# Residual through the w transforms of a spectral block, run as four 64x64 tiles, in an attention and FFT kernel

## The chip, the cores and the metric

The kernel runs on one core of one Trainium2 chip. The metric is device microseconds, the median over runs of one launch. Before the change it is 3665.09 us over 3 runs (3663.27 to 3667.23).

## The reference, cut to what matters

`x` is [2, 48, 48, 768] float32: two images of 48 x 48 pixels (2304 tokens) and 768 channels. Two layers follow each other, each a residual around a group norm (32 groups) and a body:

```python
x = x + attention(_gn(x))      # 12 heads of 64, relative positions in h and w, then @ proj_w + proj_b
x = x + spectral(_gn(x))

def spectral(x):               # B, H, W, C = 2, 48, 48, 768; nb, bs = 8, 96
    xf = rfft2(x, axes=(1, 2), norm='ortho')              # [2, 48, 25, 768], complex
    xr, xi = (p.reshape(B, Hf, Wf, nb, bs) for p in (xf.real, xf.imag))
    o1r = gelu(einsum(xr, w1[0]) - einsum(xi, w1[1]) + b1[0])
    o1i = gelu(einsum(xi, w1[0]) + einsum(xr, w1[1]) + b1[1])
    o2r = softshrink(einsum(o1r, w2[0]) - einsum(o1i, w2[1]) + b2[0], 0.01)
    o2i = softshrink(einsum(o1i, w2[0]) + einsum(o1r, w2[1]) + b2[1], 0.01)
    return irfft2(o2r + 1j * o2i, s=(48, 48), norm='ortho')
```

Each einsum multiplies the 96 channels of one of 8 blocks by a 96x96 matrix. A two-dimensional transform is done as two one-dimensional ones, over w (48 points to 25 complex values) and over h.

## The kernel before

**Order of the work.** Attention for both images comes first (24 pairs of heads, 18 units each). Then, image by image, the output projection with the residual (`project_out`) and the spectral layer (`Spectral`). Nearly all matmuls are float32, which the trace shows as two records per matmul. Instructions are issued to each engine in program order where an `InOrder` wrapper is used (`pr.sync`, `pr.pool`, `self.sync`); the others may be put in another order by a scheduler that works with estimated costs.

**`project_out`, one image.** 18 tiles of 128 tokens, in 6 groups of three. For each group `tokens` loads the attention output `oT` (128 channels on the partitions) and the inverse softmax sums `inv` by SP's queue, and GpSimd multiplies them. For each tile and each half of 384 output channels, `product` accumulates six matmuls in a PSUM bank `acc`. The residual rows of `x` lie in six tiles `x2[i]` of [96, 4, 768]: two image rows of 48 pixels on 96 partitions, four such pairs along the free dimension. `rows(i)` loads one, and GpSimd adds the projection bias `pb`. VectorE adds `acc` into `x2` (L941); since 128 tokens and 96 pixels do not match, `shifts(t)` cuts each `acc` into three pieces (108 adds per image). As soon as two pairs of rows are complete, `over_w` transforms them over w: four matmuls per call with the constant `fw` (96 x 112, block diagonal for the two image rows) on 192 channels of two row pairs, so 384 columns (`ps_y`, L920). ScalarE copies the result to `y1`, and SP stores it to DRAM as `y_d` (L929). For the last tile the two channel halves are transformed and stored one after the other.

**Where things lie.** `x2` stays in SBUF to the end of the image: it also collects the output. For the first image the projection's weights `w`, bias `pb` and two of the three token buffers lie in the large buffer `span`, the first tokens in buffers left from attention; for the second image everything but two token buffers lies in a region `po_r` ("room") which is loaded while the first image's spectral layer ends.

**`Spectral`, one image.** The channels are worked in 8 blocks of 96, `n = 0..7`, two blocks to a slice `s` of 192 channels. `load` brings five pieces `y2` of a slice from `y_d`, which puts h on the partitions. Per block: `over_h` (25 matmuls into `ps_z`, squares for the group norm on ScalarE), `mean` and `norm` (small VectorE operations, among them L1071 and L1073, then the sums `both` on GpSimd), `first` (the block's `w1` in a three-multiplication complex product, Gelu), `second` (`w2`, bias, soft shrink: VectorE makes a clipped value, GpSimd subtracts it, L1177). In the second block of each slice `back_h` follows two pieces behind: the transform back over h (`ps_u`), and a store to `u_d` (L1199). Block n's `over_h(n+1)` runs before `second(n-1)` and `first(n)`.

`back_w(s)` is the transform back over w: for each of six `u2` tiles of [100, 4, 192] it runs two matmuls with `iw` (100 x 96, `ps_x`, L1213), VectorE adds the result into `x2` (L1221), and SP stores those rows of that slice to `out`. It also loads the `u2` tiles of the next slice. It is called at the end of the turns n = 2 (which only loads the tiles of s = 0), 4, 6 and 8 (s = 0, 1, 2), and for s = 3 at the end.

**`prepare`.** `prepare(False)`, at n = 7, opens the second image's projection: first tokens and weights are loaded by SP. `prepare(True)`, before the last `back_w`, runs what is left of its steps.

## Time and profile before

| | |
|---|---|
| median of 3 runs | 3665.09 us (3663.27 to 3667.23) |
| the profiled execution | 3660.19 us, of which its span is 3658.4 |
| mean granted TensorE clock in the span | 0.987 |
| busy: TensorE, VectorE, ScalarE, GpSimd | 97%, 79%, 70%, 56% |
| DMA | 607.61 MB, 166 GB/s over the span |
| attention of both images | 0 to about 2838 us |
| projection of image 0, last `acc` | 2838.0 to 2984.2 |
| first `first` of image 0 | 3010.3 |
| last `ps_x` of image 0 | 3236.5 |
| projection of image 1, last `acc` | 3236.5 to 3405.4 |
| first `first` of image 1 | 3430.0 |
| last store of `u_d`; end of the span | 3634.37; 3658.4 |

How to read the views: PE is TensorE's matmuls, PEld its weight loads (beside the matmuls), DVE VectorE, ACT ScalarE, POOL GpSimd, SP the engine that issues most DMAs. A group's line names the source line, engine, operation, the tiles written and read, the tile shape that TensorE uses (rows*columns), the operand shapes and the count; then the busy time, the mean of one in ns, and the idle time of the engine just before, with what ended it. A row of the chain of waits has its start and duration in us and the engine or DMA that the end of the span waited for. A row of the stretches has its limits and length, the busy time of PE, PEld, DVE, ACT and POOL with instructions in brackets, the granted clock (1 is full speed), the busy share of the 16 DMA engines, and GB/s. Matmul records in a stream overlap, so the mean of one is longer than what one adds to the stream.

### The profile page before, as it was taken

To read this page: it belongs to the slowest core of one execution; us is meant where nothing else is said; L and a number is where in the kernel's file an instruction comes from. 1 tells how busy PE (TensorE), PEld (TensorE's weight loads), DVE (VectorE), ACT (ScalarE), POOL (GpSimd) and SP (SyncE) were. 2 spreads that over 40 slices of the span, in tenths; PEclk is the share of its full clock that TensorE was granted. 3 is DMA by queue.
4 is the path that set the end of the run, shared out by engine and by line. 5 is a ranking of instruction groups with operands and counts; after the bars stand their busy time and mean duration, and the time that the engine had idled before them with its cause. 6 is when DMAs were issued, how large, how long until landed. Compare 5 with 4: busy or idle time off the path is not lost.

```text
span 3658.4 us, 92606 instructions
## 1 busy us (share of the span) xinstructions
PE 3548.6 (97%) x36032; PEld 2477.2 (68%) x36032; DVE 2902.1 (79%) x6771; ACT 2557.2 (70%) x3769; POOL 2047.2 (56%) x662
## 2 busy tenths in 40 slices
PE   7999999999999999999999999999988999999898
PEld 5677676767767666677676767767666557655675
DVE  4798989989989996799898989899996437743576
ACT  3788888888888888688888888888885124301342
POOL 2567666757575763567666666666673524343232
PEclk9999999999999999999999999999999989999999
DMA  3687778777777885677777777777888743585434
GB/s 105 142 181 171 180 171 179 172 179 171 181 169 175 214 200 122 140 178 174 176 176 171 177 173 175 176 176 172 188 190 190 200 127 85 169 213 147 109 110 140
DMA packets 496484, 607.61 MB, mean 166 GB/s; under 512 B 179117, under 2 KB 311597, under 8 KB 496046
## 3 DMA queue, kind: packets, MB, share of 16 engines
q1 hardware_dynamic: 496046, 601.68, 69.3%
q8 instruction: 286, 4.69, 0.6%
q14 instruction: 152, 1.25, 0.1%
HBM read 131.60 MB, written 87.67 MB: 60 GB/s over the span
## 4 chain that ended last, share of the span: by engine, by line
PE 84%; DVE 5%; ACT 3%; DMA 3%; issue 2%; POOL 1%; SPq 1%; POOLq 0%; DVEq 0%; ACTq 0%
PE ps_o L68 22%; PE ps_s L68 21%; PE ps_proj L68 15%; PE ps_v L68 8%; PE acc L68 7%; DVE s L68 2%; PE ps_u L1195 2%; PE ps L1160 2%; PE ps_y L920 2%; PE ps_r L68 2%; SPq L68 1%; PE ps_x L1213 1%; DMA pT<-s 1%; ACT spectrum L1035 1%; POOL s L68 1%
## 5 line engine op out<-in xcount | busy, mean ns | idle before, releaser
L68 POOL TENSOR_TENSOR s<-rhw 128x2304 f32<-128x2304 f32 x432 | 1740.8, 4062 | 1025.3 <-DMA pT<-s 546.8
L68 DVE CUSTOM_DVE_ANT_0 s<-ps_s,s 128x512 f32<-128x512 f32 (+1 forms) x2160 | 1222.2, 633 | 299.7 <-issue 196.1
L68 ACT ACTIVATE s<-s,nm 128x1152 f32<-128x1152 f32 x864 | 1074.7, 1245 | 335.3 <-DVE nm L68 333.1
L68 DVE STREAM_TRANSPOSE s<-s 128x1152 f32<-128x1152 f32 x864 | 1112.0, 1344 | 6.8 <-ACT s L68 6.8
L68 ACT COPY pT<-s 32x1152 f32<-32x1152 f32 x864 | 993.6, 1150 | 25.9 <-PE ps_o L68 7.5
L68 PE MATMUL ps_o<-pT,v 128*64 128x128 f32 x15552 | 906.5, 276 | 41.7 <-ACT res L68 18.9
L68 PEld LDWEIGHTS ps_o<-pT,v 128*64 128x64 f32 x15552 | 875.4, 139 | 84.0 <-issue 43.6
L68 PE MATMUL ps_s<-kT,qT 64*128 64x512 f32 (+1 forms) x4320 | 899.8, 554 | 4.9 <-DVE mx L68 1.7
L68 PEld LDWEIGHTS ps_s<-kT,qT 64*128 64x128 f32 x4320 | 432.3, 186 | 418.1 <-issue 347.0
L68 PE MATMUL ps_proj<-xnT,w 128*64 128x384 f32 (+1 forms) x4032 | 591.3, 446 | 4.9 <-ACT xnT L68 3.7
L68 PEld LDWEIGHTS ps_proj<-xnT,w 128*64 128x64 f32 x4032 | 281.0, 137 | 278.8 <-issue 212.1
L941 DVE TENSOR_TENSOR x<-acc,x 32x384 f32<-32x384 f32 (+2 forms) x216 | 119.2, 553 | 227.8 <-PE acc L68 163.8
L68 PE MATMUL ps_v<-w,xnT 128*64 128x128 f32 x5184 | 297.3, 274 | 0.0
L68 PEld LDWEIGHTS ps_v<-w,xnT 128*64 128x64 f32 x5184 | 281.7, 137 | 21.2 <-DVE mx L68 21.2
L927 ACT COPY y<-ps_y 112x384 f32<-112x384 f32 x96 | 46.0, 479 | 299.5 <-PE ps_y L920 282.7
L68 DVE DVE_READ_ACCUMULATOR2_ANT mx<- 128x1 f32 x2160 | 179.7, 83 | 0.0
L68 ACT ACTIVATION_READ_ACCUMULATOR s<-s,nm 128x1 f32 x864 | 161.4, 187 | 0.0
L1177 POOL TENSOR_TENSOR spectrum<-spectrum 128x480 f32<-128x480 f32 x80 | 96.3, 1204 | 113.2 <-DVE spectrum L1176 85.0
L1160 PE MATMUL ps<-w,spectrum 96*64 96x96 f32 x3200 | 143.1, 248 | 0.0
L1160 PEld LDWEIGHTS ps<-w,spectrum 96*64 96x64 f32 x3200 | 133.6, 137 | 11.1 <-issue 4.4
L68 PE MATMUL acc<-proj_s 128*128 128x384 f32 x360 | 118.2, 486 | 0.4 <-POOL x L68 0.4
L68 PEld LDWEIGHTS acc<-proj_s 128*128 128x128 f32 x360 | 68.3, 190 | 48.2 <-POOL x L68 0.6
(139 smaller groups left out, 2299.8 us busy)
## 6 DMA issues: line engine op xcount, KB each, us to landing
pT<-s SPq DMA_DIRECT2D x2592, 144.0 KB
t<-rel SPq DMA_DIRECT2D x144, 189.0 KB
rhw<-t SPq DMA_DIRECT2D x144, 144.0 KB
y<-y_d SPq DMA_DIRECT2D x40, 360.0 KB
u_d<-spectrum SPq DMA_DIRECT2D x40, 360.0 KB
u<-u_d SPq DMA_DIRECT2D x48, 300.0 KB
w<-in_qkv_w SPq DMA_DIRECT2D x36, 384.0 KB
oT<-res SPq DMA_DIRECT2D x72, 192.0 KB
```

The source lines that it names most:

```text
L68: return lambda *args, **kw: self.tc.keep_in_program_order(op(*args, **kw))
L920: nc.tensor.matmul(ps[:YP, : 2 * SC], lhsT=k.fw, rhs=part[:, t0 : t0 + 2, ch], start=True, stop=True,)
L927: nc.scalar.copy(y1[:, :, ch], ps[:YP, : 2 * SC].rearrange("p (t c) -> p t c", c=SC))
L941: nc.vector.tensor_tensor(dst, acc[p : p + n, :UQ], dst, ALU.add)
L1035: self.nc.scalar.activation(junk, part, AF.Square, accum_out=total)
L1160: nc.tensor.matmul(ps[64 * r : 64 * r + 64, w * BS : (w + 1) * BS], lhsT=self.o1[:, ri, f0 : f0 + 64], rhs=w2[:, (0, 2, 1, 0)[2 * r + ri], ...
L1177: nc.gpsimd.tensor_tensor(val, val, clip, ALU.subtract)
L1195: nc.tensor.matmul(ps[: 2 * HW, :480], lhsT=k.ih, rhs=d2[:, c0 : c0 + 480], start=True, stop=True)
L1213: nc.tensor.matmul(ps[: 2 * HW, : 2 * SC], lhsT=k.iw, rhs=self.u2[s, i][:, t : t + 2, :], start=True, stop=True,)
```

## The change

The residual is no longer kept in SBUF. The transform over w and the one back over w give the identity together, so the transformed residual `yy`, which is read again from `y_d`, is added to `u2` before the transform back, and its result is the output.

- **Layout.** An image row lies on 64 partitions instead of 48: of each pair of rows, row 0 on partitions 0 to 47, row 1 on 64 to 95 (its first 32 pixels) and 112 to 127 (the others), the last 16 pixels of both rows lie side by side on 32 to 63 and again on 96 to 127, and `fw` is zero for the copy that a row does not use. `rows` loads a group of eight image rows with five DMAs (48, 16, 32, 16, 16 partitions) into a tile [128, 4, 768], three buffers in rotation. In attention the token order within a group is changed to match (`finish`, `send`, the latter with two more DMAs); the last group of the last pair and its inverse sums go by ScalarE's queue. `moves` cuts three to five pieces of an `acc` (156 adds per image).
- **Forward.** `fw` is 64 wide, twice on the partitions. Each `over_w` does, for each half of 384 channels, two by two matmuls on 64x64 tiles: input rows 0 to 63 and 64 to 127, output columns 0 to 63 and 64 to 127 (8 matmuls of 384 columns instead of 4). ScalarE copies and, itself, issues two stores of 50 partitions. For the last group the three tiles' first halves come first, then their second halves, with the `over_w` calls between; only the last call, on half the channels, stands behind the last product.
- **Backward.** `u2` and `yy` are [128, 8, 192] tiles, three each for the whole kernel, image row parity on the upper and lower 64 partitions, each loaded by two DMAs of 50 partitions (`fetch`). For s = 0 to 2 GpSimd adds `yy` to `u2` (`residual`: three adds of 128x1536 at n = 3, 5, 7), one turn after the loads; the transform follows at the next `back_w`, whose results are copied by VectorE and ScalarE in turn to `ot` tiles (three buffers) and stored by two DMAs per tile. For s = 3 the sum is made in PSUM: `yy` and `u2` are both multiplied and accumulated, for two or three pairs of banks with `yy` ahead of `u2` (`early`).
- **Around it.** GpSimd's clips and `both` are issued in program order; `mean(0)` and `norm(0)` come one piece earlier in image 0's and image 1's `over_h(1)`; the constants are loaded once; `y2` has 10 buffers instead of 8; the second image's `w` and `pb` change places in the region; two product halves of the second image run in `prepare(True)`; six GpSimd fills clear the new tiles once.

```diff
 def moves(t):
+    done = 0
+    for p in range(0, P, 32):
+        k, m = divmod(t % 3 * 4 + p // 32, 3)
+        if p >= done:
+            n = min(P, p + 96 - 32 * m) - p if p in (0, 64) and m == 0 else 32
+            yield p, n, k, 32 * m
+            done = p + n
+        if m == 1:
+            yield p, 32, k, 96
...
     def rows(g):
-        part = x2[i]
-        pr.sync.dma_start(out=part, in_=x_v[:, i * XP : (i + 1) * XP, :])
-        for j in range(XP):
-            pr.pool.tensor_tensor(part[:, j, :], part[:, j, :], pr.pb[:R], ALU.add)
+        part = rows_pool.tile([P, 4, C], F32, tag="x1", name="x1")
+        x1[g] = part
+        sync = nc.sync if pr.room is not None and g < 2 else pr.sync
+        for q, i, w0, n in (
+            (0, 0, 0, 48), (48, 1, 32, 16), (64, 1, 0, 32), (96, 0, 32, 16), (112, 1, 32, 16),
+        ):
+            sync.dma_start(out=part[q : q + n], in_=x_v[g, i, w0 : w0 + n])
+        for j in range(4):
+            pr.pool.tensor_tensor(part[:, j, :], part[:, j, :], pr.pb, ALU.add)
...
+    def over_w(n, halves=range(2)):
+        g, k0 = n // 2, 2 * (n % 2)
+        y1 = work.tile([P, 2, C], F32, tag="y1", name="y1")
+        for hf in halves:
+            cols = slice(hf * UQ, (hf + 1) * UQ)
+            both = [bank(f"ps_y{i}") for i in range(2)]
+            for c in range(2):
+                for i in range(2):
+                    r = slice(64 * i, 64 * i + 64)
+                    pr.pe.matmul(
+                        both[i][64 * c : 64 * c + 64, :UQ],
+                        lhsT=k.fw[r, :],
+                        rhs=x1[g][r, k0 + c, cols],
...
+            for i in range(2):
+                nc.scalar.copy(y1[:, i, cols], both[i][:, :UQ])
+        cols = slice(halves[0] * UQ, (halves[-1] + 1) * UQ)
+        for c in range(2):
+            nc.scalar.dma_start(
+                out=y_v[2 * n + c, :, :, cols], in_=y1[64 * c : 64 * c + 2 * KW, :, cols]
             )
-        pr.sync.dma_start(out=y_d[:, 2 * g : 2 * g + 2, ch], in_=y1[:, :, ch])
...
+    for t in range(NT - 3):
...
+        if t % 3 == 2:
+            over_w(2 * g)
+        elif t % 3 == 0 and g:
+            over_w(2 * g - 1)
+    c = HW // 4 - 1
+    for hf in range(2):
+        for t in range(NT - 3, NT):
+            outputs(t, hf)
+            if t == NT - 3:
+                if hf:
+                    over_w(c, (0,))
+                else:
+                    over_w(c - 2)
+        over_w(c - 1, (hf,))
+    over_w(c, (1,))
...
+    def fetch(self, tiles, src, j):
+        for i in range(2):
+            self.sync.dma_start(
+                out=tiles[j][64 * i : 64 * i + 2 * KW], in_=src[i][..., j * XP : (j + 1) * XP, :]
+            )
+
+    def rows_of(self, j, q, both, terms, first=True, last=True):
+        pe, k = InOrder(self.tc, self.nc.tensor), self.k
+        for x, of in enumerate(terms):
+            for m in range(2):
+                for i in range(2):
+                    r = slice(64 * i, 64 * i + 2 * KW)
+                    t = XP // 2 * m + 2 * q
+                    pe.matmul(
+                        both[i][64 * m : 64 * m + 64, : 2 * SC],
+                        lhsT=k.iw[r, :],
+                        rhs=of[j][r, t : t + 2, :],
+                        start=first and x == 0,
+                        stop=last and x == len(terms) - 1,
...
     def back_w(self, s, more, early=0):
+        last = s == NBK // NB - 1
...
+        if more:
+            ch = slice((s + 1) * SC, (s + 2) * SC)
+            u_v = self.u_d.rearrange("w (i r t) c -> i w r t c", i=2, r=2)
+            for j in parts:
+                self.fetch(self.yy, self.y_d.rearrange("(q i) t c -> i q t c", i=2)[..., ch], j)
+        for j in parts if s < 0 else ():
+            self.fetch(self.u2, u_v, j)
+        for turn in turns[:early]:
+            ahead[turn] = banks()
+            self.rows_of(*turn, ahead[turn], [self.yy], last=False)
+        for j, q in turns:
...
+                self.rows_of(j, q, both, [self.yy, self.u2] if last else [self.u2])
...
+            for i in range(2):
+                self.copy(
+                    ots[j][:, 2 * q : 2 * q + 2, i, :],
+                    both[i][:, : 2 * SC].rearrange("p (t c) -> p t c", c=SC),
                 )
...
+                if more:
+                    self.fetch(self.u2, u_v, j)
+                for m in range(2):
+                    self.sync.dma_start(
+                        out=self.out_v[j, m, :, :, s * SC : (s + 1) * SC],
+                        in_=ots[j][64 * m : 64 * m + HW].rearrange("p t i c -> p (t i) c"),
+                    )
+    def residual(self):
+        for u2, yy in zip(self.u2, self.yy):
+            self.pool.tensor_tensor(u2, u2, yy, ALU.add)
...
             elif i == 0:
                 self.back_w(s - 2, True)
-        self.prepare(True)
-        self.back_w(s - 1, False)
+            elif s:
+                self.residual()
+        held = self.prepare(True)
+        self.back_w(s - 1, False, early=2 if held else 3)
```

## The prediction

> **What bounds the kernel now.** I read the page first (which engine carries the chain), then stretches of the span, the groups by form, the chain of waits in time order, and single lines and DMA answers for prices.
>
> ```profile
> span 3658.4 us, 92606 instructions
> ...
> PE 3548.6 (97%) x36032; PEld 2477.2 (68%) x36032; DVE 2902.1 (79%) x6771; ACT 2557.2 (70%) x3769; POOL 2047.2 (56%) x662
> ...
> PE ps_o L68 22%; PE ps_s L68 21%; PE ps_proj L68 15%; PE ps_v L68 8%; PE acc L68 7%; DVE s L68 2%; PE ps_u L1195 2%; PE ps L1160 2%; PE ps_y L920 2%; PE ps_r L68 2%; SPq L68 1%; PE ps_x L1213 1%; DMA pT<-s 1%; ACT spectrum L1035 1%; POOL s L68 1%
> ```
>
> TensorE is the chain, and attention (up to about 2838 us) is most of it. The change works in the last 820 us, where its targets `ps_y` and `ps_x` stand on the chain. The stretches of the two output projections, the first entry into the spectral stage, and the tail:
>
> ```profile
> 2838.00:2984.20 146.20, 144.91 (x449) 83.99 (x450) 53.00 (x96) 21.08 (x45) 59.16 (x33) 1.00 0.65 167
> 3236.30:3405.40 169.10, 167.95 (x521) 97.47 (x520) 58.08 (x106) 21.09 (x44) 67.76 (x29) 1.00 0.69 166
> ```
> ```profile
> 2975.00:3000.00 25.00, 19.59 (x98) 13.79 (x97) 6.54 (x12) 8.64 (x21) 2.18 (x3) 0.89 0.73 187
> 3000.00:3025.00 25.00, 21.43 (x153) 16.66 (x152) 13.43 (x42) 14.69 (x37) 5.10 (x5) 0.70 0.30 75
> ...
> 3625.00:3658.40 33.40, 24.86 (x104) 11.15 (x102) 17.64 (x32) 2.22 (x4) 2.41 (x2) 0.98 0.68 212
> ```
>
> Columns are PE, PEld, DVE, ACT, POOL busy, clock, DMA share, GB/s. The projections are TensorE-bound at full clock with DMA at 0.65 to 0.69; the entry loses both busy time and clock (0.70); the tail is moved by DMA at 212 GB/s.
>
> ```profile
> L920 PE MATMUL ps_y<-x,fw 96*112 96x384 f32 x192 | 66.8, 487 | 4.6 <-DVE x L941 4.6
> L1213 PE MATMUL ps_x<-u,iw 100*96 100x384 f32 x192 | 66.7, 499 | 7.9 <-DMA u<-u_d 6.6 <-DVE x L1221 1.3
> ```
> ```profile
> 2989.11 5.27 DMA y<-y_d
> 2994.52 6.56 PE ps_z L1100 x40
> 3019.03 4.33 PE ps_z L1100 x50
> ```
> ```profile
> 3103.19 1.78 PE ps_u L1195 x4
> 3117.91 7.74 PE ps_x L1213 x24
> ```
>
> From the chain: a 384-column record takes 7.74/24 = 0.3225 us in a stream, and a matmul is two records, 0.645 us. `ps_z` at the entry costs 0.164 us a record against 0.087 later: the low clock.
>
> **1. Forward w transforms.** Before, an image has 48 matmuls (96 records): 31.0 us on TensorE. After, 96 matmuls on 64x64 tiles, 192 records. How many run side by side is not in this trace for four tiles; for two it is:
>
> ```profile
> 1001.59 2.42 PE L68 MATMUL ps_s<-kT,qT 64*128 64x512 f32 x10
> ```
>
> Ten 512-column records alone would need 10 x 0.430 = 4.3 us; two row halves together took 2.4. With four at once 192 x 0.3225/4 = 15.5 us; with two, 31.0 again. I take four, since row halves (`ps_s`) and column halves (`ps_proj`, 4032 records in 591 us, 0.147 each) both overlap fully. A switch of shape costs: four `ps_u` records of 480 columns should take 1.61 us and took 1.78 between `ps` column halves, so (1.78 - 1.61)/2 = 0.085 per switch; 28 switches per image at just under 0.1 are 2.7 us. [...] Gain: 2 x (31.0 - 15.5 - 2.7) = **-25.6** (bounds -26 and +5).
>
> Beside it, hidden: DVE adds rise from 108 to 156 per image at 0.553 us (L941), 86 us in 133; with no such room the extra 27 us would count. ScalarE issues 28 stores at SP's 0.3 to 0.4 us, 10 us beside 21 busy. Six zero fills on GpSimd lie between 0.1 us (the 96x32 fill) and 48 times that each, at most 35 us beside 59 of 146. In attention two more small DMAs per `send`, 24 times, are 38 us of SP's queue over 2800 us (three took 2.40), and nobody waits for `inv_d` soon. Constants of the second image are no longer loaded, which was off the chain.
>
> **DMA cover.** The new transfers touch 48, 50, 32 or 16 partitions instead of 96 to 128. In one group's 17 us (rates in 40 slices):
>
> ```profile
> GB/s 220 394 398 231 29 148 311 329 361 351 249 192 184 202 184 184 239 253 206 220 192 221 184 217 206 224 231 239 267 224 210 224 224 239 275 405 412 419 328 275
> ```
>
> The `oT` tokens on 128 partitions run at 310 to 400, the `inv` broadcast on 64 at 184 to 250, `x` on 96 at 206 to 267, the 112-partition `y_d` store at 400. [...] Rows alone: 32-partition `pT` copies ran at 222 GB/s, so 16 partitions lie between 222 and half that. Of `x` (1.57 MB per group) the 48- and 32-partition pieces, 0.98 MB, take 4.4 us, the three of 16, 0.59 MB, 2.7 to 5.3: 7.1 to 9.7 against 5.2 (1.18 MB at 227). The `y_d` stores (1.23 MB) take 3.4 to 5.6 (360 to 220 GB/s) against 3.4. Six groups add 11 to 40: DMA time per image goes from 0.65 x 146 = 95 us and 0.69 x 169 = 117 to 106..135 and 128..157, against TensorE's 133 and 156. **+6** (0 to +14).
>
> **2. Backward w transforms.** `back_w` for s=0 and 1 stands on the chain at 7.74 us (24 records); after, 48 records at a quarter: 3.9 plus two switches, -3.7. Four times: **-14.8** (+1 if only two tiles overlap). DVE's 12 adds of 0.553 become 12 copies split with ScalarE, less than before. For s=2 and 3 DMA decides, see 5 and 6.
>
> **3. Entry.** Now the last `acc` ends at 2984.2 and 3405.4, `first(0)` starts at 3010.3 and 3430.0. SP holds the loads behind the `y_d` store of the other half (2989.11). After, the store is ScalarE's, and half 0 is finished 9 us of TensorE work earlier: `over_h(0)` and (1), 4.3 us each, and `norm(0)`, 6 us, put `first(0)` 16 us after `acc`: -10. In image 1 four of five pieces share memory with the projection weights and wait for the last product: -5. `mean` and `norm` one piece earlier are in this. **-15** (-8 to -20).
>
> **4. GpSimd adds.** 128x480 takes 1.204 us and 128x2304 5.05, so 128x1536 takes 3.4, three 10.3 us, at n=3, 5, 7. GpSimd is otherwise idle 11 us or more before the next clip at n=3 and 5. But:
>
> ```profile
> L1071 DVE TENSOR_TENSOR nm_rstd<-nm_rstd,nm_fit x48: 145/155/1203, 3007.5 to 3584.1; 96x1 f32<-96x1 f32 x48
> L1073 DVE TENSOR_SCALAR w<-w,nm_rstd x16: 412/416/944, 3009.7 to 3584.8; 96x288 f32<-96x288 f32 x16
> ```
>
> These DVE lines stretch to a GpSimd add's whole length (1203 ns). At n=3 the norm's last L1071 and L1073 (3087.2, 3087.4) follow the last clip (3084.7 to 3085.9), where the adds now start: up to 5.5 us during which `first`'s evictions queue behind them on DVE; seven banks soak up part. I take 2.5 each, four times: **+10** (0 to +20). At n=7 GpSimd is idle 6.75 us before the clip of 3619.18, so it comes 3.5 late, and `back_h` waits: **+3.5** for image 1 (0 to 5); image 0's is in 5.
>
> **5. Handover to image 1.** Now `ps_x` ends at 3236.5, six product halves (3.87 each) carry TensorE to 3259.7. After: two halves run earlier, `ps_x` is shorter, 6 us of TensorE idle can go. Against that DMA carries 3.7 MB of `yy` more (18 us at 200 GB/s), halves of `u` and `out` at two thirds of the speed, and `x` rows: `u` lands 9 to 18 us later than 3235, then four halves: 3261 to 3270, and up to 10 more with the rows ahead of it. **+6** (-5 to +18).
>
> **6. Tail.**
> ```profile
> 3634.37 0.30 SPq L1199 DMA_DIRECT2D u_d<-spectrum  x1
> 3637.37 0.29 SPq L68 DMA_DIRECT2D u<-u_d  x1
> ```
> From here 5.4 MB of `u`, out(2), out(3) end the span at 3658.4. After, `yy` is pinned behind that `u_d` store: 7.2 MB, 24 to 29 us at 250 to 300 GB/s (mixed loads and stores do better than one kind), 36 at 200. It uses the 3 us in which SP waits. **+8** (+3 to +14).
>
> Sum: -25.6+6-14.8-15+10+3.5+6+8 = **-21.9** on 3658.4, a span of 3636.5. The profiled execution took 3660.19, 1.8 over its span, and the median of the runs, 3665.09, lies 4.9 above that: **3643**.
>
> **Rivals.** *Everything hides*: terms 4 and DMA cover at zero, handover -5, tail +3, entry -15: -57, or halfway, **3618**. For it: DMA share is only 0.65; against: every price above has a row. *Narrow transfers bind* (slower): a projection group has 25.8 us of TensorE; DMA's 135 and 157 are 22.5 and 26.2 a group. Above 25.8 it decides; at 28.5, 12 groups cost 12 x 2.7 = 32, with handover +18, tail +14 and entry -8: +29, **3694**. For it: the 64-partition row at half speed. *Two tiles at once*: terms 1 and 2 give +5 and +1: +25, **3690**; against it the full overlap of both halves. *Terms cancel*: 3655 to 3672, DVE stalls at 5 each with entry -10.
>
> **How the numbers follow.** Forecast 0.48 (3625 to 3660), hidden 0.20, narrow transfers 0.15, two tiles 0.07, cancel 0.10. About 0.2%, 7 us, is what a measurement tells from no change. Faster: 0.46+0.20 = 0.66; same 0.10; slower 0.15+0.07+0.02 = 0.24. Range 3606 to 3688: it leaves out the far ends of the first and last cases. Forecast alone: 3625 to 3660.
>
> **What would show it.** Right: `ps_y` records start in fours, 1.3 us per `over_w`; projections of 133 to 140 and 156 to 164 us; clock near 1 at both entries; L1071 above 2 us at n=3 and 5; tail of 26 to 33 us after the last `u_d` store. Wrong: `ps_y` at 2.6 us per `over_w`, `acc` waiting for GpSimd `x` or DMA, or a tail as short as now.

## The result: 3.3% slower, and the profile after

The changed kernel takes 3784.95 us (median of 4 runs, 3780.39 to 3790.82) against 3664.18 us: ratio 1.033, interval [1.0312, 1.0348]. The forecast was 3643, with a range up to 3688. The profiled execution took 3786.28 us, its span is 3784.5, 126.1 longer than before. The page of the changed kernel, span, busy times and chain:

```profile
span 3784.5 us, 94042 instructions
...
PE 3570.9 (94%) x36512; PEld 2466.1 (65%) x36512; DVE 2968.2 (78%) x6819; ACT 2573.9 (68%) x3817; POOL 2114.7 (56%) x686
...
PE 82%; DMA 5%; DVE 5%; issue 3%; SPq 2%; POOL 2%; ACT 2%; ACTq 0%; POOLq 0%; DVEq 0%
```

No engine is fuller than before. TensorE's share falls from 97 to 94%; its busy sum rises by 22 us although the transforms are cheaper, and the granted clock falls from 0.987 to 0.963. DMA goes from 3% to 5% of the chain. The 126 us are waits, so they are looked for by stage. The table gives the length of each stage in us, read from the trace's records; "spectral" runs from the first `ps_1r` record of `first(0)` to that of `first(7)`, "last block" from there to the issue of the last `u_d` store, "wait" from that store to the last `ps_x`:

| stage | before | after | difference |
|---|---|---|---|
| attention, to the first `acc` | 2805.7 | 2808.3 | +2.7 |
| projection 0 | 178.6 | 191.6 | +13.0 |
| entry 0 | 27.4 | 31.8 | +4.4 |
| spectral 0 | 179.8 | 198.8 | +19.0 |
| last block 0 | 24.7 | 45.0 | +20.3 |
| wait 0 | 20.4 | 40.1 | +19.7 |
| rest of projection 1 | 169.1 | 162.5 | -6.6 |
| entry 1 | 25.9 | 26.3 | +0.5 |
| spectral 1 | 178.9 | 199.8 | +20.9 |
| last block 1 | 24.1 | 36.1 | +12.1 |
| wait 1 | 19.2 | 37.3 | +18.1 |
| last `ps_x` to the end | 4.9 | 6.8 | +1.9 |

Differences are taken before rounding. The `ps_1r` record stands 1.4 us behind the first record of `first(0)`, which is the one that the prediction's 3010.3 names. Attention's 2.7 us cannot be told from what one run differs from another: the kernel before varies by 12 us from run to run.

What was forecast as gain is there where TensorE works without waits. TensorE's timeline in the projection of image 0 (start, length, tile, shapes, records):

```profile
2927.59 1.52 PE L67 MATMUL ps_y<-x,fw 64*64 64x384 f32 x16
```

The same product among the groups of instructions, in the window from 2820 us on (busy us, mean ns, then the idle time before it and what ended it):

```profile
L67 PE MATMUL ps_y<-x,fw 64*64 64x384 f32 x384 | 53.0, 523 | 24.7 <-DVE x L970 24.7
```

Sixteen records add 1.45 us to the stream (from 2927.59 to the next product at 2929.04), against 2.58 for the eight that they replace (2902.74 to 2905.32 before): four tiles do run side by side, and 12 calls save 13.6 us per image. The 24.7 us of idle time in the group's line, waiting for VectorE's `x`, is the first hint of where this went.

**Spectral, n = 3.** The chain of waits around `first(3)`, and GpSimd's timeline beside it:

```profile
3105.36 0.04 DVE nm_rstd L1121
3105.40 12.72 issue
3118.11 0.57 DVE spectrum L1191
3118.68 0.04 issue
3118.72 1.65 PE ps_1i L1185 x2
```
```profile
3106.86 1.19 POOL L67 TENSOR_TENSOR spectrum<-spectrum 128x480 f32<-128x480 f32 x1
3108.01 3.41 POOL L67 TENSOR_TENSOR u__29563<-u__29563,yy__29566 128x1536 f32<-128x1536 f32 x1
3111.39 3.41 POOL L67 TENSOR_TENSOR u__29564<-u__29564,yy__29567 128x1536 f32<-128x1536 f32 x1
3114.76 3.41 POOL L67 TENSOR_TENSOR u__29565<-u__29565,yy__29568 128x1536 f32<-128x1536 f32 x1
```

The chain calls it "issue", but VectorE is inside one instruction: L1121, the 96x1 product that was L1071 before. That line's own record has its worst case (the middle number is the median, the third the longest, in ns):

```profile
L1121 DVE TENSOR_TENSOR nm_rstd<-nm_rstd,nm_fit x48: 145/436/12840, 3026.5 to 3681.9; 96x1 f32<-96x1 f32 x48
```

It begins while GpSimd runs `both`, and ends when the last add ends (3114.76 + 3.41 = 3118.17; VectorE's next instruction starts at 3118.11). So it was held through the rest of `both`, a clip and all three adds. `first(3)`'s evictions (L1191) stand behind it, and TensorE waits 10 us for a bank. The same happens at n = 5, and at both places in the second image. It is the second of the norm's three such products, and it was caught by `both`, 2.6 us before the first add; the prediction had its last one meet the adds.

**Last block.** GpSimd's timeline of image 1 at n = 7; the brackets give the idle time before an instruction and what ended it:

```profile
3705.23 1.20 POOL L67 TENSOR_TENSOR spectrum<-spectrum 128x480 f32<-128x480 f32 x1 [0.44 <-PE ps_1r L1185]
3707.45 3.46 POOL L67 TENSOR_TENSOR u__29563<-u__29563,yy__29566 128x1536 f32<-128x1536 f32 x1 [1.02 <-DMA u__29565<-u_d]
3713.49 3.44 POOL L67 TENSOR_TENSOR u__29564<-u__29564,yy__29567 128x1536 f32<-128x1536 f32 x1 [2.58 <-DMA u__29564<-u_d]
3719.77 3.42 POOL L67 TENSOR_TENSOR u__29565<-u__29565,yy__29568 128x1536 f32<-128x1536 f32 x1 [2.84 <-DMA u__29565<-u_d]
3723.14 3.51 POOL L67 TENSOR_TENSOR spectrum<-spectrum 128x480 f32<-128x480 f32 x3
```

The adds wait for the `u` loads issued just before, and the last block's clips, which follow them in GpSimd's program order, wait with them: three clips run in one go at 3723.14.

**Wait.** SP's queue after the last `u_d` store:

```profile
3740.42 0.30 SPq L1249 DMA_DIRECT2D u_d<-spectrum  x1
3740.82 1.78 SPq L67 DMA_DIRECT2D yy__29566<-y_d  x2
3742.70 1.64 SPq L67 DMA_DIRECT2D yy__29567<-y_d  x2
3744.43 3.55 SPq L67 DMA_DIRECT2D yy__29568<-y_d  x2
3748.08 2.44 SPq L67 DMA_DIRECT2D u__29563<-u_d  x2
```

First `yy`, then `u`; the last `u` lands at 3773.6. Before, six `u` loads were issued in the first 10 us.

**Projection 0.** The chain after attention's last product:

```profile
2840.97 0.26 ACT turned L67
2841.24 0.02 issue
2841.26 6.93 DMA inv_d<-turned
2848.18 0.02 issue
2848.20 6.49 DMA x<-in_x
```

The first `x` rows are issued at 2840.24, where the kernel before issued them at 2818.30; of the 21 us from 2840 to 2861 TensorE is busy for 3.5.

### The profile page after: what moved, and what is told of

It reads as the page before. It is cut to its first block, busy times and chain, and to the rows that moved or that the text cites. A ratio compares the mean times of both kernels' runs of the same rounds, so it can differ in the third digit from the quotient of the medians.

```text
span 3784.5 us, 94042 instructions
## 1 busy us (share of the span) xinstructions
PE 3570.9 (94%) x36512; PEld 2466.1 (65%) x36512; DVE 2968.2 (78%) x6819; ACT 2573.9 (68%) x3817; POOL 2114.7 (56%) x686
## 4 chain that ended last, share of the span: by engine, by line
PE 82%; DMA 5%; DVE 5%; issue 3%; SPq 2%; POOL 2%; ACT 2%; ACTq 0%; POOLq 0%; DVEq 0%
PE ps_o L67 21%; PE ps_s L67 20%; PE ps_proj L67 14%; PE ps_v L67 8%; PE acc L67 7%; PE ps L1210 3%; DVE s L67 3%; PE ps_z L1150 2%; SPq L67 2%; PE ps_r L67 2%; DMA pT<-s 1%; PE ps_y L67 1%; DMA u__29565<-u_d 1%; PE ps_u L1245 1%; PE ps_1i L1185 1%
## 5 line engine op out<-in xcount | busy, mean ns | idle before, releaser
L970 DVE TENSOR_TENSOR x<-acc,x 32x384 f32<-32x384 f32 (+2 forms) x312 | 173.0, 554 | 181.7 <-POOL x L67 104.6
L957 ACT COPY y<-ps_y 128x384 f32<-128x384 f32 x96 | 40.0, 490 | 289.4 <-PE ps_y L67 289.3
L67 POOL TENSOR_TENSOR spectrum<-spectrum 128x480 f32<-128x480 f32 x80 | 96.1, 1203 | 226.0 <-DVE nm_total L1108 116.4
L1192 ACT ACTIVATE spectrum<-spectrum,b 96x400 f32<-96x400 f32 x96 | 57.8, 625 | 83.3 <-DVE spectrum L1191 83.1
```

Source lines behind the costliest of these rows:

```text
L67: return lambda *args, **kw: self.tc.keep_in_program_order(op(*args, **kw))
L957: nc.scalar.copy(y1[:, i, cols], both[i][:, :UQ])
L970: nc.vector.tensor_tensor(dst, acc[p : p + n, :UQ], dst, ALU.add)
L1192: nc.scalar.activation(o1, o1, AF.Gelu, bias=self.b1[:, n, ri : ri + 1])
```

## Experiments

The kernels are the changed one with the edit named, unless said otherwise; a time without an interval is one run, and the stage lengths come from its profile. The kernel before, beside them, took between 3656.8 and 3669.1 us.

### 1. GpSimd's adds left out

```diff
     def residual(self):
-        for u2, yy in zip(self.u2, self.yy):
-            self.pool.tensor_tensor(u2, u2, yy, ALU.add)
+        return
```

> The changed kernel with GpSimd's three residual adds at n = 3, 5 and 7 left out (the output then lacks the residual on channels 0 to 575); loads, transforms and stores are as they were. Theory A (the adds themselves: at n = 3 and 5 they hold VectorE's 96x1 product for 12.7 us, and at n = 7 they stand in GpSimd's order ahead of the last block's clips): first(3) to first(4) goes from 42.4 and 43.7 us back to about 30, first(5) to first(6) from 41.7 and 42.4 to about 30, and the last u_d store comes 10 to 17 us sooner after first(7): 80 us less in all, 3705 us. Theory B (the new narrow transfers set the pace, the adds only fill time in which loads are awaited): the four stalls at n = 3 and 5 go (about 50 us) but the stretch from first(7) on stays as long, since it waits for u2: 3735 us.

Measured 3718.81 us, 66 less. `first(3)` to `first(4)` is 30.1 in both images (42.4 and 43.6 after), `first(5)` to `first(6)` 30.1 and 30.1 (41.7 and 42.4): 49.9 us in four stalls. The last block is 36.3 and 26.3 instead of 45.0 and 36.1: 18.5 more. The longest L1121 is down to 1.56 us. The four stalls cost what both theories say. At n = 7 the adds cost 8.7 and 9.8 us, just below theory A's 10 to 17 and not the nothing of B; the time lies between A's 3705 and B's 3735. In image 1 the last block is then nearly that of before; in image 0 11.7 us stay, and the waits behind the last `u_d` store (38.1 and 35.1) move by 2 us.

### 2. The adds cut into 24

```diff
         for u2, yy in zip(self.u2, self.yy):
-            self.pool.tensor_tensor(u2, u2, yy, ALU.add)
+            for t in range(XP):
+                self.pool.tensor_tensor(u2[:, t, :], u2[:, t, :], yy[:, t, :], ALU.add)
```

> Each of GpSimd's residual adds is cut into eight of 128x192, so 24 short instructions instead of three of 3.4 us. If VectorE is let in between two GpSimd instructions, its 96x1 product waits 1 us at most and first(3) to first(4) and first(5) to first(6) fall by about 11 us each, 45 us in all: 3740 us. If VectorE is held until GpSimd's run of back-to-back instructions ends, the product lasts as long as before, 12 us or somewhat more (24 fixed costs instead of 3): 3785 to 3800 us.

Measured 3789.37 us. GpSimd's timeline at the same place, and VectorE's line:

```profile
3108.18 4.41 POOL L67 TENSOR_TENSOR u__29563<-u__29563,yy__29566 128x192 f32<-128x192 f32 x8
3112.54 4.42 POOL L67 TENSOR_TENSOR u__29564<-u__29564,yy__29567 128x192 f32<-128x192 f32 x8
3116.90 4.44 POOL L67 TENSOR_TENSOR u__29565<-u__29565,yy__29568 128x192 f32<-128x192 f32 x8
```
```profile
L1121 DVE TENSOR_TENSOR nm_rstd<-nm_rstd,nm_fit x48: 144/460/15832, 3027.5 to 3688.6; 96x1 f32<-96x1 f32 x48
```

Twenty-four instructions of 0.55 us hold VectorE off even longer, 15.83 us against 12.84, by just the 3 us that they take more. So at these four places VectorE was not let in between GpSimd instructions that follow each other without a gap. Before, L1071 was held for at most 1203 ns, the length of one clip, and that looked like the price of one instruction.

It is not so at every place. In the changed kernel, 2 us before the long wait, the norm's first product meets the end of a clip:

```profile
3102.73 1.20 POOL L67 TENSOR_TENSOR spectrum<-spectrum 128x480 f32<-128x480 f32 x1 [0.44 <-DVE nm_rstd L1116]
3103.89 3.00 POOL L67 TENSOR_TENSOR both<-spectrum 96x400 f32<-96x400 f32 x3
```
```profile
3103.35 0.59 DVE L1121 TENSOR_TENSOR nm_rstd<-nm_rstd,nm_fit 96x1 f32<-96x1 f32 x1
```

It ends with the clip, though `both` follows without a gap. Of the 24 records of L1121 longer than 0.3 us, 18 were let in like this at the end of the one instruction that they met, two waited 1.6 us, to the end of the next one, and only the four ahead of the adds waited for the whole run. What decides between the two is not shown.

### 3. The whole residual in PSUM

```diff
     def back_w(self, s, more, early=0):
...
-            for j in parts:
+            for j in parts if s < 0 else ():
                 self.fetch(self.yy, ...)
...
-                self.rows_of(j, q, both, [self.yy, self.u2] if last else [self.u2])
+                self.rows_of(j, q, both, [self.yy, self.u2])
...
                     self.fetch(self.u2, u_v, j)
+                    self.fetch(self.yy, y_v, j)
     def residual(self):
+        return
```

> The sum of residual and spectral part is made in PSUM for all four slices, as the changed kernel does for the last one; GpSimd adds nothing, yy of the next slice is loaded tile by tile behind the matmuls that used the old one. Theory A: the gain of leaving the adds out, about 80 us, less 48 more records (4.0 us) at each of three back_w per image, 24 us: 3730 us. Theory B: the yy loads now stand between u2 and out in SP's queue, so the handover and the tail lose some 5 us each more: 3755 us or above.

Measured 3726.47 us, 58 less than the changed kernel. As in experiment 1 the four stalls are gone (30.1 each). The doubled backward transforms cost 3.9 us at each of n = 4 and 6 (27.8 against 23.9, 22.5 against 18.6), so that `back_w` is back at the time of before. The last block takes 29.0 and 25.5. The waits are not shorter, 39.9 and 39.3 (40.1 and 37.3 after). The time is theory A's 3730 to 4 us, in part by luck: leaving the adds out had given 66 us, not 80, and the extra transforms cost 15.6 us in the two images, not 24.

### 4. Memory of the x rows

```diff
-                o_pool, w_pool = pool("sp_o", 3), pool("sp_w", 2)
+                o_pool, w_pool = pool("sp_o", 3) if b else None, pool("sp_w", 2)
...
                 z_pool = z_pool or pool("sp_z", 1)
+                o_pool = o_pool or pool("sp_o", 3)
```

> One pool (ot, 18 KB) of the first image is opened after its projection instead of before, so that the pool of the x rows ends at address 177728 instead of 196160: below the last attention tiles (pT) and below the y2 tiles. Theory M (the first x load at 2840.2 waits for the last ps_o, and the y2 loads at 3003.9 for the last ps_y, only because the pools share memory): x is issued at about 2821, TensorE's gap from 2840 to 2861 shrinks by 15 to 20 us, and the entry into the spectral stage of image 0 from 31.8 to about 24: 25 us less, 3760 us. Rival N (ten transfers on 16 to 48 partitions at 131 GB/s and the stores by ScalarE set these times): both stay within 5 us, 3780 us.

Measured 3777.15 us. Entry 0 goes from 31.8 to 22.6: the `y2` loads had waited for the last `ps_y` only because their pool overlapped that of the `x` rows. Projection 0 gains 6.2, so the entry is as M has it and the projection is not. Projection 1 loses 8.8: `ot` of image 0, in use to its end, now lies where image 1's rows go, and their load is issued behind the last stores of `ot`. SP's queue shows why the first gain is small:

```profile
2829.16 17.87 SPq L67 DMA_DIRECT2D x<-in_x  x5
```

`x` now starts at 2829, but the third of its five transfers is issued at 2836.95, when the first has landed, and the fourth at 2846.24: it waits 9.0 us for the landing of an `oT` store that ScalarE issues at 2844.36, after attention's last unit. In the changed kernel's trace the 3586 transfers of SP and ScalarE use eight semaphores, 448 or 449 times each, and 2748 of the issues wait on their own one, so for the landing of an earlier transfer; there the third piece of `x` uses the semaphore that the late `oT` store had. A load of five pieces takes five turns at them, the wide load one.

### 5. The same, with the last attention stores on SP

```diff
-                o_pool, w_pool = pool("sp_o", 3), pool("sp_w", 2)
+                o_pool, w_pool = pool("sp_o", 2), pool("sp_w", 2)
...
-            return act if (pr, g) == (pairs - 1, HW // 8 - 1) else sync
+            return sync
```

(on top of experiment 3)

> The sum in PSUM for all slices, and two edits at the first image's projection: two ot buffers instead of three, so that the pool of the x rows ends at 190016, below the last attention tiles and the y2 tiles, in both images; and the last attention stores (oT and the inverse sums) back on SP's queue. In the run with ot opened later, x's second to fifth transfer stood 9 us behind the landing of an oT store that ScalarE issues late. Theory M2 (that wait, not the transfers' speed, keeps x from the first projection): x of the first group has landed by 2838, the first projection takes 170 to 176 us instead of 191.7, and the entry 23 instead of 31: 3700 us. Rival N: x lands after 2845 all the same, the projection keeps 185 us: 3712 us.

Measured 3731.41 us, 5 above experiment 3, which is within what single runs differ by: M2's edit does not help. Entry 0 is 22.8, but projection 0 stays at 193.8, as N says of it, and with two `ot` buffers `back_w` costs 4 to 5 us more at n = 4 (32.1 and 32.6). The reason is again the place in the queue: SP issues one `x` piece at 2828.34, then at 2843.37 the `oT` store that waits for attention's end, and the other four from 2847.64 on: the load of five pieces was split by the schedule, where one wide load could not be.

### 6. The transfers by themselves

> No part of the layers: only the transfers, each kind by itself and one after the other, of the old and of the new forms (y_d stores on 112 partitions by SP, on 50 by ScalarE; u loads on 100 partitions and in halves of 50; yy loads, in pieces of 768 bytes, on 100 partitions and in halves of 50; x on 96 partitions and in five pieces; out on 96 partitions and in halves of 48; halves once from SP alone and once from SP and ScalarE). Theory P (transfers inside half of the partitions are slow): halves from one queue run at 0.5 to 0.7 of the wide form's GB/s, whatever the size of their pieces, and halves from two queues at nearly the wide rate, since both halves are then in flight. Rival Q (pieces of 768 bytes are slow, partitions do not matter): u halves as fast as u wide, yy slow on 100 partitions too. Rival R (the transfers are as fast as before, only their order in SP's queue is bad): all halves within 10% of the wide forms.

Nine of the stretches of this kernel (no engine works beside DMA but a few markers on VectorE), in order: `y_d` stores on 112 and on 50 partitions; `u` on 100 partitions, in halves from SP, in halves from SP and ScalarE; `yy` in halves from SP, and from both; `x` on 96 partitions and in five pieces. The last two numbers are the busy share of the 16 DMA engines and GB/s:

```profile
34.80:62.70 27.90, 0.09 (x5) 0.00 (x0) 1.00 0.86 296
62.80:103.30 40.50, 0.12 (x4) 0.00 (x0) 1.00 0.55 182
112.50:123.00 10.50, 0.87 (x10) 0.00 (x0) 1.00 0.47 176
...
133.60:151.30 17.70, 0.96 (x10) 0.00 (x0) 1.00 0.26 104
151.40:169.50 18.10, 0.90 (x8) 0.00 (x0) 1.00 0.27 102
169.60:183.20 13.60, 0.89 (x6) 0.00 (x0) 1.00 0.55 136
183.20:194.00 10.80, 0.96 (x9) 0.00 (x0) 1.00 0.53 171
194.10:206.60 12.50, 0.19 (x4) 0.00 (x0) 1.00 0.82 189
206.70:228.80 22.10, 0.60 (x7) 0.00 (x0) 1.00 0.95 142
```

None of the three theories covers all of it. The shares name the main one: `u` in halves keeps 0.26 of the DMA engines busy. The packet records agree: on average 4.9 packets in flight for `u` halves, 9 to 10 for the other transfers on 50 partitions and for those on 100, 14 to 15 for those on 96 and 112, and 15.8 for `x` in five pieces. A 6144-byte packet takes 234 ns in `u` halves as in the old `y_d` stores, so the packets are not slower, there are fewer at a time. `u` halves are read as 25 groups of two rows, `yy` halves as 50 rows; experiment 8 reads `u` as 50 rows too. The five-piece `x` is another matter: all engines are busy (0.95), but a 3072-byte packet takes 327 ns where it takes 211 in the wide load. There the cut form does cost; whether by the fewer partitions or by the number of transfers in flight is not separated. `yy` in halves lies between, and reaches the rate of the wide form (177 GB/s, the stretch left out) when two queues issue the halves; `u` does not.

### 7. The last slice's yy ahead of time

```diff
+                t_pool = t_rooms.enter_context(tc.tile_pool(name="sp_t", bufs=1, side="right"))
...
-                self.prepare(False)
+                self.tail = self.prepare(False)
+                for j in range(HW // 2 // XP):
+                    self.fetch(self.tail, y_v[..., (NBK // NB - 1) * SC :], j)
```

(three more tiles, loaded at n = 7, on top of experiment 5; the fills are gone)

> As before it, and the last slice's yy has three tiles of its own, loaded at n = 7 instead of behind the last u_d store (the clearing fills are left out as well, since nothing reads the rows they clear). Theory T (the 1.84 MB of yy stand in the way between the last u_d store and the last transform): from that store to the last ps_x 25 to 28 us instead of 39, in both images, 25 us less than the kernel without this edit: 3675 us. Rival P2 (u halves and out halves alone are slow enough): 33 to 35 us, 10 us less in all: 3690 us.

Measured 3712.59 us, 19 less than experiment 5. The waits are 34.3 and 31.4 instead of 42.2 and 38.5: 8 and 7 us, and nearer to P2's 33 to 35 than to T's 25 to 28, though image 1's is below P2's; the 19 us lie between the two theories. `yy` in the way is a good third of what experiment 5 loses there against the kernel before (21.8 and 19.3).

### 8. u_d laid out to be read as 50 rows

```diff
-            self.u_d = self.dp.tile([KW, 2 * HW, SC], F32, tag="u_d", name="u_d")
+            self.u_d = self.dp.tile([2, KW, HW, SC], F32, tag="u_d", name="u_d")
...
-            u_v = self.u_d.rearrange("w (i r t) c -> i w r t c", i=2, r=2)
+            u_v = self.u_d.rearrange("i w (r t) c -> i (w r) t c", r=2)
```

(on top of experiment 7; `back_h` stores two halves)

> The kernel of yy3_sp with u_d laid out by row parity first ([2, 25, 48, 192] instead of [25, 96, 192]), so that a half of u2 is read as 50 equal rows instead of 25 groups of two; back_h stores two halves of 48 partitions. In the transfers by themselves u halves had 4.9 packets in flight and 131 GB/s, yy halves (50 rows) 10.1 and 164, and two queues did not help u. Theory E (a transfer is dealt out to the DMA engines by its outermost count: 25 gives 5 of 16, 50 gives 10): from the last u_d store to the last ps_x 8 us less in both images (26 and 23 instead of 34.3 and 31.4), the rest of the spectral stage a few us less, 20 us in all: 3690 us. Rival P (half of the partitions is the limit): no change there, 3710 us.

The waits fall to 26.2 and 22.3, by 8 and 9 us, as theory E has it, and n = 4 takes 28.6 and 28.2. Of the 6144-byte packets of the last `u` loads five are mostly in flight at once in experiment 7's trace (4.1 on average) and ten in this one (8.2), so reading `u` as 50 rows instead of 25 groups is worth that part. The time, 3721.46 us, is nevertheless 9 higher: the last block of image 0 takes 48.3 us instead of 30.0, and projection 0 and its entry are 4.5 and 5.6 us longer in this one run, for which no run shows the reason. GpSimd there:

```profile
3235.13 5.03 POOL L67 TENSOR_TENSOR proj<-proj 128x2304 f32<-128x2304 f32 x1 [42.53 <-DMA proj<-inv_d]
3240.12 5.82 POOL L67 TENSOR_TENSOR spectrum<-spectrum 128x480 f32<-128x480 f32 x5
```

Five clips stood behind the second image's token product, whose `inv` load SP had issued late: the program order on GpSimd, without any residual add.

### 9. The first x rows by ScalarE, into free memory

```diff
-            sync = nc.sync if pr.room is not None and g < 2 else pr.sync
+            sync = nc.scalar if g == 0 and first is not None else ...
```

(on top of experiment 8; the first group lies in two `u2` tiles at the lowest address)

> As u_lay, and the first image's first x group goes to the memory of two u2 tiles (the lowest of this stage, free before attention ends) by ScalarE's queue, ahead of the last attention stores. Theory M2 (x comes late because of memory and of its place behind those stores): x has landed before 2840, the gap of TensorE from 2840 to 2860 goes, the first projection takes 172 to 177 us instead of 191, 15 us less than u_lay: 3675 us. Rival N (the speed of the five narrow transfers, also of the second group): 186 us or more, 3686 us.

Measured 3702.12 us, 19 less. Projection 0 takes 179.1 instead of 195.5, and from 2876 to 2992 TensorE is busy for 115.25 of 116 us. M2's cause holds. The length is still that of before, not 13 less: the adds of the first group (GpSimd from 2845 on, its own product first) still keep TensorE for some 5 us, and the granted clock between 2836 and 2876 is 0.91.

### 10. GpSimd free again

```diff
-        self.sync, self.pool = InOrder(tc, tc.nc.sync), InOrder(tc, tc.nc.gpsimd)
+        self.sync, self.pool = InOrder(tc, tc.nc.sync), tc.nc.gpsimd
```

(on top of experiment 9)

> As u_x0, but GpSimd's clips and sums of the spectral stage are no longer held in program order. In u_lay and u_x0 the clips of the last block of image 0 stood behind the second image's token product on GpSimd (3235 to 3240), which waits for a late load: first(7) to the last u_d store took 48 us there and 25.8 in image 1. Theory G (the order on GpSimd): that stretch falls to 26 to 30 us, 20 us less in all: 3682 us. Rival S (SP's queue holds the u_d stores back): 45 us or more, 3700 us.

Measured 3690.11 us, 12 less; the last block of image 0 falls from 48.4 to 33.0, 15 of the 20 us of theory G and not quite to its 26 to 30. All repairs together take 95 us of the 121 away, and the kernel is still 29 us slower than the kernel before in the same series of runs (3661.22).

### 11. and 12. The forward part alone

The kernel before with the change's layout, `moves`, `over_w` and order of the last group; its own `back_w` with `iw` spread on 128 columns. Experiment 12 also moves the second image's first `x` rows to ScalarE's queue, and in the last `back_w` lets ScalarE store some of the pieces of `out`.

```diff
-        pr.sync.dma_start(out=part, in_=x_v[:, i * XP : (i + 1) * XP, :])
+        sync = nc.scalar if early and g == 0 else pr.sync
+        for q, i, w0, n in (
+            (0, 0, 0, 48), (48, 1, 32, 16), (64, 1, 0, 32), (96, 0, 32, 16), (112, 1, 32, 16),
+        ):
+            sync.dma_start(out=part[q : q + n], in_=x_v[g, i, w0 : w0 + n])
...
-                self.sync.dma_start(
-                    out=self.out_v[:, i * XP : (i + 1) * XP, ch], in_=part[:, :, ch]
-                )
+                for q, r, w0, n in ((0, 0, 0, 48), (64, 1, 0, 32), (112, 1, 32, 16)):
+                    self.sync.dma_start(
+                        out=self.out_v[i, r, w0 : w0 + n, :, ch], in_=part[q : q + n, :, ch]
+                    )
```

> The kernel before with the forward part of the change alone: rows on 64 partitions in five loads, order of tokens, forward transforms as four 64x64 tiles, ScalarE's y_d stores, last group by halves; the residual stays in SBUF as before, VectorE adds the spectral part to it, back_w is as before with its result spread on 128 partitions, and out is stored in pieces of 48, 32 and 16 partitions. The first x group is loaded by ScalarE's queue. Theory F (the forward tiles gain 12.6 us per image where TensorE is busy, and nothing else of the change gains): projections of 168 and 158 to 160 us instead of 178.6 and 169.1, entries of 22 to 27 us, tail and handover 3 to 6 us longer by the smaller pieces: 3640 to 3655 us, faster than before. Rival D (the narrow loads and stores and VectorE's 156 adds eat the forward gain as well): 3664 us or slower.

> As fwd, but the first x group of the second image is also loaded by ScalarE's queue (in fwd SP issues it behind 18 stores of out, TensorE then waits 8 us at 3261 to 3269 and runs at clock 0.78 in the 20 us around it), and in the last back_w of the last image ScalarE stores the pieces of 32 and 16 partitions. Theory F2 (fwd's forward gain is there and lies under these waits): projection of image 1 at 162 to 165 us instead of 173.1, end 5 instead of 7.9 us after the last ps_x; 3658 to 3664 us, the same as before or slightly faster. Rival D2 (TensorE is slowed throughout by transfers or by VectorE): 170 us or more, 3670 us.

Measured 3672.56 us, ratio 1.0029 [1.0017, 1.0042], and 3674.94 us, ratio 1.003 [1.0019, 1.0042]. The spectral stages are those of before to 1 us. Attention takes 8.0 and 4.6 us longer in these two profiles; how much of that is the two more small transfers of each `send` and how much one run's difference from another is not shown. Projection 0 takes 179.0 and 181.7 us against 178.6, projection 1 173.1 and 171.5 against 169.1, the entries 22.1 and 26.8 in experiment 11, and in experiment 12 the last wait is 26.4 instead of 19.2. Its first stretches in experiment 11, PE, PEld, DVE, ACT, POOL, clock, DMA share and GB/s, and the same of the kernel before:

```profile
3236.00:3256.00 20.00, 19.30 (x61) 11.14 (x60) 2.23 (x4) 0.00 (x0) 5.05 (x1) 1.00 0.92 233
3256.00:3276.00 20.00, 12.32 (x32) 5.01 (x31) 6.59 (x12) 0.54 (x2) 7.08 (x4) 0.78 1.07 159
```
```profile
3236.00:3256.00 20.00, 20.00 (x64) 11.78 (x63) 0.97 (x2) 0.00 (x0) 5.05 (x1) 1.00 1.03 234
3256.00:3276.00 20.00, 20.00 (x64) 11.67 (x63) 13.68 (x25) 1.92 (x4) 14.19 (x8) 1.00 1.09 203
```

At the same DMA share the kernel before gets 203 GB/s and its `x` in time; here 159, GpSimd adds the first bias 9 us later (3266.72 against 3258.05, of which 2 are a later start of the stage), TensorE idles and the clock drops. With ScalarE's queue (experiment 12) the bias comes at 3263.92 and the clock in 3260 to 3280 is 0.66; the gain stays away. D and D2 come out in size, but by the start of the projection rather than "throughout": in experiment 12 TensorE is busy for 99.93 of the 100 us from 3300 to 3400.

TensorE's timeline at the start of experiment 11's first projection shows a second reason, which lies in the order of the work:

```profile
2849.51 0.83 PE L67 MATMUL ps_y<-x,fw 64*64 64x384 f32 x2 [2.98 <-issue]
2853.62 4.81 PE L67 MATMUL ps_y<-x,fw 64*64 64x384 f32 x12 [0.86 <-DVE x L967]
2858.36 8.01 PE L67 MATMUL acc<-proj_s 128*128 128x384 f32 x24
```

The changed kernel calls the first `over_w` directly behind the third tile's product, where the kernel before has the 24 records of the next product in between (`acc` at 2838.15, `ps_y` at 2845.96). So TensorE now waits there for GpSimd's bias and VectorE's adds: from 2846.5 to 2858.36 for 1.45 us of work, some 10 us, and in the second image from 3262.6 to 3278.05, some 14 us. That is about the size of the whole forward gain of 13.6 us per image. A kernel with the old place of `over_w` was not tried. So no kernel tried here beats the one before.

## Why the prediction was wrong, step by step

**1. Forward transforms: right** in price (1.45 us per call against a forecast of 1.29, or 1.52 with the switches; 13.6 us per image against 12.8). **DMA cover, +6: wrong**, in its place. It was sized by the mean DMA time of a group against TensorE's 25.8 us, and inside the groups that holds (118.89 of 119 us busy from 2876 to 2995). What it left out is the first group, which has no earlier group to hide under. Projection 0 lost 13.0 where 13.6 should have been gained: 26.6 us. Experiments 4, 5 and 9 show a cause, memory shared with attention's last tiles and a load of five pieces behind stores that wait for attention's end; 12.5 us came back when both were taken away (191.6 to 179.1). The rest stays open; experiment 11's first `over_w`, which waits some 10 us for its operand, is a likely part. Projection 1 took 162.5 us, within the 156 to 164 forecast, but by luck: two product halves of 8.0 us had left it for the handover. Counting them it is +1.4 instead of -13.6; there experiments 11 and 12 show late and slower `x` loads and a low clock.

**2. Backward transforms: right.** n = 4 and 6 went from 27.4 and 22.4 to 23.9 and 18.6, 14.5 us in all against 14.8.

**3. Entry, -15: wrong.** It was +4.4 and +0.5. The step "half 0 is finished 9 us earlier" held, but the `y2` loads were issued at 3003.86, after the last `ps_y`. The prediction had looked at shared memory for image 1 only. Experiment 4 gave the 9 us back in image 0.

**4. GpSimd adds, +10 and +3.5: the step that failed.** The mechanism was the one named, VectorE's small product held by GpSimd, and nearly the place; the size was wrong. "Up to 5.5 us during which `first`'s evictions queue", taken at 2.5, was 12.8 us of holding four times, and leaving the adds out gave 49.9 us back, some 12.5 each (experiment 1), since at these places VectorE's instruction was held until GpSimd's whole run had ended (experiment 2). Of each 12.8 us the seven banks soaked up some 2.8, so that TensorE stood for 10.0; behind that the granted clock was 0.50 (3115 to 3125), which fits the 2.5 us more that a stall cost. Had VectorE waited for one instruction only, as the 1203 ns of L1071 before suggest, experiment 2 would have shown stalls of one short add, about 0.6 us, and it showed 15.8. Most of the shorter waits do end with one instruction (18 of the 24 above 0.3 us, experiment 2). At n = 7 the adds cost 8.7 and 9.8, not 3.5: the prediction took GpSimd's time and left out that the adds wait for `u` loads that have only just been issued, with the clips in program order behind them.

**5. Handover, +6, and 6. Tail, +8: mechanism right, size wrong.** Measured +32.0 (20.3 + 19.7, less the 8.0 of the two product halves that moved into it) and +32.1 (12.1 + 18.1 + 1.9), of which the adds of n = 7 are 8.7 and 9.8. The tail was sized as 7.2 MB at 250 to 300 GB/s. After the last `u_d` store the rate was 193 GB/s at a DMA share of 0.64: of `u`'s 6144-byte packets five were most often in flight at once, 3.7 on average. The prediction went by the number of partitions and did not look at the outermost counts. Its two thirds of the speed for halves was an estimate: in experiment 6's kernel `u` halves ran at 104 of 176 GB/s, `out` halves at 194 of 211 (issued by SP alone, then by SP and ScalarE). Loads and stores mixed did better than either alone for `u` and `out` in the wide form: 253 GB/s together before (3637 to 3658.4), 176 and 211 by themselves in experiment 6's kernel. Experiments 7 and 8 split the 18.1 us of the last wait: about 7 for `yy` in the way, about 9 for reading `u` as 25 groups instead of 50 rows.

Of the rivals, "narrow transfers bind" had the right sign and the right resource, at the wrong place: it was priced in the projection's groups, where TensorE hides it, and not where nothing runs beside the transfers. "Everything hides" has a slip: its own terms add up to 3608, halfway to the forecast 3625, not 3618; it was wrong by either.

The span was 148 us above the forecast one (3784.5 against 3636.5). By stage some 55 of them are the adds, 34 the two projections, 32 the handover and the tail without the adds, and 20 the entries; no other stage is off by more than 5.

**What stays open.** Why a 3072-byte packet to 16 or 32 partitions takes 327 ns instead of 211 was not separated from how many such transfers are in flight. What lets VectorE in between two GpSimd instructions at one place and not at another is not known. Where the first `over_w` stands was not varied. Of the 29 us by which experiment 10 is slower, the stage lengths give 16 to the handover (last block and wait of image 0) and 6 to image 1's last block, wait and end; which part of it is the order in SP's queue and which the speed of the transfers was not tried. Its projections take 180.1 and 169.5 us, so neither keeps its forward gain, and attention is 4 us longer.

## What to carry to other kernels

Here an operation of GpSimd beside VectorE cost at worst the whole gapless run that it became part of, not only its own length (12.84 us of holding with adds of 3.41): reckon with that price where the longest run can meet a VectorE instruction, and ask for every instruction that is moved on an in-order queue what is behind it and what it waits for. When a step is moved forward in the busiest engine's order, ask whether its operand is there by then. A saving on the busiest engine is worth its full price only in the stretches where that engine never waits: first and last groups, where no other work covers a transfer, have to be costed by themselves. When a transfer is cut or its layout changed, look at its outermost count (`u` kept mostly five packets in flight with 25, ten with 50), at the number of turns that it takes at the eight semaphores (five for `x` in pieces, one in the wide form), and at whose memory it lands in.

## What the runs showed of the hardware

- VectorE's 96x1 product of two SBUF operands was held for 12.84 us by a gapless run of GpSimd instructions up to the end of three adds of 3.41 us, and for 15.83 us when the adds were 24 of 0.55 us (four times each). Of the 20 other waits above 0.3 us in the changed kernel, 18 ended with the GpSimd instruction that was met, though the next followed without a gap.
- Packets in flight differed with the form of the transfer: 4.9 for `u` halves, read as 25 groups (104 GB/s over the stretch), 9 to 10 for the other transfers on 50 partitions and for those on 100, 14 to 15 for those on 96 and 112. With the same `u` read as 50 rows instead of 25 groups of two, mostly ten packets were in flight instead of five.
- Two queues brought two 50-partition `yy` halves from 136 to 171 GB/s, but left `u` halves at 102.
- The clock was lower around the end of a wait of TensorE. In experiment 11 it idled for 7.7 us of 3256 to 3276, and the granted clock was 0.50 for 10.2 us (3267.0 to 3277.2); in experiment 12 it idled for 4.6 us of 3260 to 3280, and the clock was 0.50 for 13.6 us (3266.2 to 3279.8). The means of these 20 us are 0.78 and 0.66.
